# One block's four token sums on VectorE: two of them issued two readings later, two of them issued in the next product

## The chip, the cores and the metric

The kernel runs on one core of one Trainium2 chip. The metric is the time on the device of one execution, in microseconds; three executions of the kernel before took 588.06, 588.19 and 589.07 us, so its median is 588.19 us. Engine names below: PE is TensorE, DVE is VectorE, ACT is ScalarE, POOL is GpSimd, SP is the engine that issues most DMAs.

## The reference

`x` has 2 x 2048 tokens of 512 numbers; all is float32. One conditioned block is computed:

```python
emb = jnp.dot(jax.nn.silu(t), ada_w) + ada_b
shift_msa, scale_msa, gate_msa, shift_mlp, scale_mlp, gate_mlp = jnp.split(emb, 6, axis=-1)
norm = _ln(x) * (1.0 + scale_msa[:, None]) + shift_msa[:, None]
h = jax.nn.gelu(jnp.dot(norm, ssm_w1) + ssm_b1, approximate=False)
ssm_out = jnp.dot(h, ssm_w2) + ssm_b2
x = x + gate_msa[:, None] * ssm_out
norm2 = _ln(x) * (1.0 + scale_mlp[:, None]) + shift_mlp[:, None]
hf = jax.nn.gelu(jnp.dot(norm2, ff_w1) + ff_b1, approximate=True)
ff_out = jnp.dot(hf, ff_w2) + ff_b2
x = x + gate_mlp[:, None] * ff_out
```

The weights are 512 x 512 (`ssm_w1`, `ssm_w2`), 512 x 1024 (`ff_w1`) and 1024 x 512 (`ff_w2`).

## The kernel before

The 4096 tokens are cut into eight blocks of 512 (numbers 0 to 7). A block passes through four matrix products, named in the program by the tile that they write: hA (the first ssm product, class `First`), oA (the second, with the residual added to `x`, function `residual`), hC (the first feed-forward product) and oC (the second, with its residual). Each is done by a scheme of the Strassen kind: the operands are cut in quarters, seven products P1 to P7 of quarters or of sums of quarters are made in place of eight, and what they give is added up again. So each product needs sums of its operands beforehand. For the ssm input of a block these are the token sums: four additions or subtractions of quarters of the normalized, modulated tokens, each 128 partitions x 512 numbers. `Norm.summed` returns them as a list of four closures that call `cut_sum` (L348). In words, with q11 to q22 the quarters:

- sum 1: s0 = q12 - q11
- sum 2: s1 = q22 - s0
- sum 3: q12 = q22 - q12, in place
- sum 4: s2 = q21 - s1

`second_operands` says which product uses which: P1 takes q11, P5 takes s0, P6 takes s1, P2 takes q21, P7 takes q12 (as sum 3 left it), P3 takes q22, P4 takes s2.

The program has no scheduler of its own: the order of the instructions on each engine is the order in which the Python code issues them. `group` (L475) issues the seven products of one matrix product, four matmuls of 256 columns each; after each product it calls `after`, which issues the readings of that product's PSUM bank, and then runs the closures that were hung on this place with `hook`. The order of the products here is `CARRIED`: P1, P5, P6, P2, P7, P3, P4. The places, however, are named in the order of `ORDER`: P1, P2, P6, P5, P7, P3, P4. So place "P2" comes after product P5, place "P5" comes after product P2, and places "P1", "P6", "P7", "P3" and "P4" come after the products of the same names.

PSUM banks are shared: P1, P6, P7 and P4 accumulate in one tile (`py`), P5 and P3 in a second (`pv`), P2 in a third (`px`). In a residual, DVE reads a bank after each product but the first and adds it to `x` (L739); ACT copies P1's bank to P2's (L489). A product that adds to a bank must wait until the reading of the product before it in this bank is done: P7 waits for P6's reading, P3 for P5's, P4 for P7's.

The change lies in one place: round i = 5 of the loop over blocks (`ahead` is true there alone). The work around it, in order of issue:

- the hC products of block 5, in whose hooks block 7's tokens are normalized (L580), turned (L591) and moved by 16 DMAs on SP (L600);
- the oA residual of block 6. Behind its product P1, ACT modulates block 7's tokens (four instructions, L623), and POOL makes the sums that oC of block 5 needs (L348). On DVE are hung block 7's four token sums and, at "P3" and "P4", four bn_stats with bn_aggr of block 6 (L512, L513);
- the hA product of block 7 (`First`, L475), which takes the token sums. ACT copies P1 (L489) and reads P5 and P6 (L682), P2 (L692) and P4 (L708); DVE reads P7 (L701) and P3 (L704);
- the oC residual of block 5 (`residual_in_leaves`, L778 and L824), at whose start POOL works out block 6's scales (L548 to L566), makes four more sums (L348), and then four of hA.

The token sums of this block are the only ones from round 1 on that DVE makes; those of the other blocks are POOL's. Before, the four stand at the places "P6", "P6", "P5" and "P7" of the residual:

Of the kernel before, what the change touches and what calls it, by code (L numbers as in the profile page):

```python
# [140 lines left out]
def kernel(  # L141
# [16 lines left out]
    nc = tc.nc  # L158
# [279 lines left out]
    def seed(name, row, part, leaf=False):  # L438


        b, cols = (("y", row[:, : D // 2]), ("v", row[:, D // 2 :]))[part]
        t = ps_g.tile([P, 2, HT], F32, tag=b, name=f"p{b}_{name}_{len(seeds.get((name, b), ()))}")
        seeds.setdefault((name, b), []).append(t)
        if part == 1 and leaf:
            nc.scalar.copy(t[:, 0, :P], cols[:, :P])
        else:
            nc.scalar.copy(t, cols.unsqueeze(1).to_broadcast([P, 2, HT]))
# [45 lines left out]
    def hook(hooks, places, ops):  # L493

        for n, op in enumerate(ops):
            hooks.setdefault(places[min(n, len(places) - 1)], []).append(op)
# [226 lines left out]
    def residual(name, i, hops, wops, kdim, hooks, last=False, order=ORDER):  # L723

        xt = xs[i]
        F = D // 2
        q = {
            "11": xt[:, 0:2, :F],
            "12": xt[:, 0:2, F:],
            "21": xt[:, 2:4, :F],  # L730
            "22": xt[:, 2:4, F:],
        }
        dest = {"P1": "11", "P2": "11", "P6": "12", "P5": "22", "P7": "22", "P3": "12", "P4": "21"}

        def after(p, ps, js):
            if p == "P1" and order is CARRIED:
                return
            d = q[dest[p]][:, js]
            nc.vector.tensor_tensor(d, ps[BANK[p]][:, js], d, ALU.add)  # L739
            if last and p in ("P7", "P4"):  # L740
                s = slice(2 + js.start, 2 + js.stop)
                f = slice(F, D) if p == "P7" else slice(0, F)
                nc.sync.dma_start(out=out_blk[i][:, s, f], in_=xt[:, s, f])

        parted = ("P1", "P6", "P7", "P4") if last else ()
        places = ORDER if order is CARRIED else None
        group(name, kdim, hops, lambda p, j, k: wops[p][:, k, :], after, hooks, parted, order, places)
# [306 lines left out]
    def run(ops):  # L1054
        for op in ops:
            op()
# [4 lines left out]
    n1 = {0: Norm(0, 1), 1: Norm(1, 1)}  # L1061
# [65 lines left out]
    n1_sums = n1[0].summed(nc.vector)  # L1127
# [17 lines left out]
    hooks = {}  # L1145
# [12 lines left out]
    hooks = {}  # L1158
# [24 lines left out]
    n1_sums = n1[1].summed(nc.vector)  # L1183
    run(st[2:3] + n1_sums[:2] + st[3:])
    hooks = {}
# [19 lines left out]
    hooks = {}  # L1205
# [14 lines left out]
    hooks = {}  # L1220
# [25 lines left out]
    hooks = {}  # L1246
# [10 lines left out]
    hooks = {}  # L1257
# [7 lines left out]
    hooks = {}  # L1265
# [12 lines left out]
    for i in range(1, NBLK):  # L1278
# [4 lines left out]
        hooks = {}  # L1283
# [43 lines left out]
        hooks = {}  # L1327
# [12 lines left out]
        if nx2:  # L1340

            hook(hooks, ("P1",) if ahead else ("P7",), n1[i + 2].moved())
            if ahead:
                hook(hooks, ("P6", "P6", "P5", "P7"), n1[i + 2].summed(nc.vector, True))
            if i == 1:
                hook(hooks, ("P1", "P1", "P2", "P6"), later[:4])
            if fold:
                hook(hooks, ("P1", "P2", "P6", "P5"), fold[5:6] + fold[4:5] + later[:2])
            oC_seeds = [lambda p=p: seed(f"oC_{i}", gb[5], p, five) for p in range(2)]
            if not ahead:  # L1350
                hook(hooks, ("P2", "P6"), oC_seeds)
            n2[i + 1] = Norm(i + 1, 2)
            hook(hooks, ("P3", "P4"), n2[i + 1].stats())
            residual(f"oA_{i + 1}", i + 1, hA[i + 1], w2_ops, KD // 2, hooks, order=CARRIED)
            if ahead:
                hooks = {}
                hook(hooks, ("P2", "P6"), oC_seeds)
                hA[i + 2] = First(i + 2, n1[i + 2].ops, hooks, CARRIED, on_act=("P6", "P5"))
        else:
            for p in EARLY:  # L1360
                run(hooks.get(p, ()))
        leaf_fold, fold = (fold or i == 1) and later[2 if fold else 4 :], None

        hooks = {}
# [63 lines left out]
        hooks = {}  # L1428
# [63 lines left out]
```

## Time and profile before

| what | us |
|---|---|
| median of three executions | 588.19 (588.06 to 589.07) |
| the profiled execution, its whole time | 588.16 |
| the same execution, first to last instruction (span) | 586.4 |
| PE busy, 430 to 457 us of the span (27 us) | 25.61 |
| DVE busy in the same stretch | 14.92 |
| ACT busy in the same stretch | 12.24 |
| POOL busy in the same stretch | 22.29 |

The last four rows are from the view by stretches of time; the oA residual of block 6 and the hA product of block 7 lie in this stretch. Times in the profile's rows are microseconds from the first instruction. Durations on PE and DVE overlap a little with the next instruction, since the engines are pipelined: DVE's readings of 0.69 us start every 0.60 us when nothing holds them, and products of eight rows (four matmuls appear as eight) last 1.89 us but start every 1.73 us. The granted TensorE clock is 0.999 of full speed.

### The profile page before, as it was taken

The page shows a single profiled execution, that of the slowest core. Times are in us where ns is not written, and L with a number is a line of the kernel's source. Part 1 is how long each engine was busy: PE and PEld are TensorE (multiplying, and loading weights), DVE is VectorE, ACT ScalarE, POOL GpSimd, SP SyncE. Part 2 cuts the span into 40 slices and gives each one's busy share as a digit, 9 for nine tenths or more (in the row PEclk, how much of TensorE's full clock was granted, in tenths as well). Part 3 has the DMA queues.
Part 4 walks back from the last instruction along what each step waited for, and adds up shares of the span by engine and source line. Part 5 has one row for each costly group of instructions (what it writes and reads, how often), then busy time and mean ns, then how long its engine had stood idle before and what let it go on. Part 6 is the DMA issues. An engine that isn't in the chain of part 4 may idle for free.

```text
span 586.4 us, 9484 instructions
## 1 busy us (share of the span) xinstructions
PE 577.9 (99%) x3303; PEld 515.5 (88%) x3303; DVE 417.9 (71%) x752; ACT 263.1 (45%) x479; POOL 428.4 (73%) x518
## 2 busy tenths in 40 slices
PE   8999999999999999999999999999999999999997
PEld 5888888888899888998889988898887998899896
DVE  4978788987867375685756857883856366787676
ACT  2234357405642554435742588226663431731420
POOL 2875359999997938969688799998688445369351
PEclk9999999999999999999999999999999999999999
DMA  8990323302205403472033721153030330031002
GB/s 317 395 393 10 91 64 82 108 37 107 55 19 178 129 1 74 113 209 72 3 90 78 282 73 29 45 141 129 19 72 1 106 113 0 1 73 72 2 1 72
DMA packets 25243, 56.49 MB, mean 96 GB/s; under 512 B 4672, under 2 KB 5740, under 8 KB 23532
## 3 DMA queue, kind: packets, MB, share of 16 engines
q1 hardware_dynamic: 21856, 51.67, 27.7%
q10 hardware_dynamic: 3340, 4.22, 3.0%
q8 instruction: 26, 0.43, 0.3%
q14 instruction: 21, 0.17, 0.1%
HBM read 32.80 MB, written 8.40 MB: 70 GB/s over the span
## 4 chain that ended last, share of the span: by engine, by line
PE 91%; DVE 3%; DMA 3%; issue 1%; ACT 0%; SPq 0%; DVEq 0%
PE px_hC L985 10%; PE py_hA L475 9%; PE py_oA L475 9%; PE py_hC L985 8%; PE py_oC L778 8%; PE pv_hC L985 8%; PE pl_oC_P_y L824 8%; PE pl_oC_P_v L824 5%; PE pv_hA L475 4%; PE pv_oA L475 4%; PE pl_oC_P_x L824 3%; DMA ada<-in_L_cond_ada_w_dram 2%; PE py_hC L475 2%; PE py_oC L475 2%; PE px_oA L475 2%; PE px_hA L475 2%
## 5 line engine op out<-in xcount | busy, mean ns | idle before, releaser
L623 ACT ACTIVATE nT<-nT,mod,mod 128x512 f32<-128x512 f32 x32 | 23.4, 803 | 56.2 <-DMA nT<-blocks 40.1
L348 POOL TENSOR_TENSOR hSC<-hClo,hChi 128x512 f32<-128x512 f32 (+1 forms) x16 | 19.7, 1235 | 38.7 <-ACT hChi L980 33.3
L512 DVE BATCH_NORM_STATS2 st<-x 128x6 f32<-128x512 f32 x60 | 40.7, 678 | 5.4 <-DMA x<-in_x_dram 5.2
L923 POOL TENSOR_TENSOR forms<-forms 128x256 f32<-128x256 f32 x56 | 41.8, 746 | 3.3
L985 PE MATMUL py_hC<-forms,fw 128*128 128x256 f32 x168 | 41.0, 380 | 0.0
L1002 DVE TENSOR_TENSOR hClo<-hClo,py_hC 128x512 f32<-128x512 f32 x42 | 28.6, 684 | 15.3 <-ACT hClo L999 9.4
L985 PEld LDWEIGHTS py_hC<-forms,fw 128*128 128x128 f32 x168 | 31.7, 190 | 4.7 <-DVE hClo L1002 0.2
L623 ACT ACTIVATE x<-x,mod,mod 128x512 f32<-128x512 f32 x24 | 17.6, 802 | 32.1 <-DMA x<-blocks 32.1
L591 DVE STREAM_TRANSPOSE blocks<-nT 128x512 f32<-128x512 f32 x32 | 22.2, 705 | 13.5 <-ACT nT L580 13.5
L923 POOL TENSOR_TENSOR forms<-nT,forms 128x256 f32<-128x256 f32 x42 | 30.5, 748 | 1.8 <-PE pl_oC_P_v L824 1.3
L923 POOL TENSOR_TENSOR forms<-nT 128x256 f32<-128x256 f32 x14 | 10.4, 740 | 29.3 <-ACT nT L623 20.4
L1002 DVE TENSOR_TENSOR hChi<-hChi,pv_hC 128x512 f32<-128x512 f32 x35 | 23.2, 681 | 10.4 <-PE pv_hC L985 6.7
L580 ACT ACTIVATE nT<-x,nmr,rstd 128x512 f32<-128x512 f32 x32 | 24.1, 806 | 13.4 <-POOL nmr L566 13.4
L985 PE MATMUL px_hC<-forms,fw 128*128 128x256 f32 x112 | 27.6, 379 | 0.0
L980 ACT ACTIVATE hClo<-hClo,colsT 128x256 f32<-128x256 f32 x56 | 25.3, 498 | 5.0 <-DVE hClo L1002 4.8
L838 DVE TENSOR_TENSOR x<-pl_oC_P_y,x 128x256 f32<-128x256 f32 (+1 forms) x66 | 24.7, 374 | 3.0 <-PE pl_oC_P_y L824 1.3
L475 PE MATMUL py_oA<-w,hA 128*128 128x256 f32 x112 | 26.5, 379 | 0.0
L999 ACT ACTIVATE hChi<-py_hC 128x512 f32<-128x512 f32 x14 | 7.6, 593 | 41.1 <-PE py_hC L985 41.0
L980 ACT ACTIVATE hChi<-hChi,colsT 128x256 f32<-128x256 f32 x56 | 25.1, 496 | 1.9 <-DVE hChi L1002 1.9
L739 DVE TENSOR_TENSOR x<-py_oA,x 128x512 f32<-128x512 f32 x26 | 17.8, 686 | 11.2 <-PE py_oA L475 10.6
L778 PE MATMUL py_oC<-fw_s,hSC 128*128 128x256 f32 x112 | 25.3, 379 | 0.0
L739 DVE TENSOR_TENSOR x<-pv_oA,x 128x512 f32<-128x512 f32 x16 | 11.0, 687 | 20.1 <-PE pv_oA L475 9.0
(339 smaller groups left out, 1796.7 us busy)
## 6 DMA issues: line engine op xcount, KB each, us to landing
x<-in_x_dram SPq DMA_DIRECT2D x13, 1024.0 KB
out_dram<-x SPq DMA_DIRECT2D x14, 512.0 KB
ada<-in_L_cond_ada_w_dram SPq DMA_DIRECT2D x6, 1024.0 KB
x<-blocks SPq DMA_DIRECT2D x96, 64.0 KB
nT<-blocks SPq DMA_DIRECT2D x80, 64.0 KB
fw<-in_L_cond_ff_w_dram SPq DMA_DIRECT2D x2, 2048.0 KB
w<-in_L_cond_ssm_w_dram SPq DMA_DIRECT2D x3, 1024.0 KB
nT<-blocks ACTq DMA_DIRECT2D x48, 64.0 KB
```

The lines of the kernel that those rows point to most:

```text
L475: nc.tensor.matmul(ps[b][j * apart][:, j, :], lhs(p, j, k), rhs(p, j, k), start=(fresh and j * (not apart) == 0 and k == 0), stop=(p in (" ...
L512: nc.vector.bn_stats(st, xs[self.i][:, c, :])
L580: nc.scalar.activation(t, x_c, AF.Identity, bias=self.nmr[:, c : c + 1], scale=self.rstd[:, c : c + 1])
L623: nc.scalar.activation(dst, src, AF.Identity, bias=shift, scale=scale)
L739: nc.vector.tensor_tensor(d, ps[BANK[p]][:, js], d, ALU.add)
L778: yield lambda j=j, k=k: nc.tensor.matmul(ps[BANK[p]][:, j, :], hops(p, j, k), wops[p][:, k, :], start=False, stop=(k == kdim - 1), skip_g ...
L824: nc.tensor.matmul(t[:, n, :], hops.leaves[p][f][:, k, :], leaf_wops[p][f][:, k, :], start=room not in started, stop=(f in ("P2", "P3", "P ...
L838: nc.vector.tensor_tensor(d, src, d, ALU.add)
L923: eng.tensor_tensor(reg[d], reg[a], reg[b], ALU.add if f == "+" else ALU.subtract)
L980: nc.scalar.activation(h, h, AF.Gelu_apprx_tanh, bias=fb1T[:, m : m + 1])
L985: nc.tensor.matmul(ps[b][:, j, :], fa[ra][:, j * P : (j + 1) * P], fb[rb].rearrange("p a (c q) -> p c a q", q=Q), start=(fresh and j == 0) ...
L1002: nc.vector.tensor_tensor(dest(d), dest(d), ps[b], op)
```

## The change

Sums 1 and 2 move to the places "P5" and "P7" of the residual, which come after the readings of the products P2 and P7. Sums 3 and 4 leave the residual and move to the places "P1" and "P2" of the hA product, which come after its first and its second product. On DVE they then stand behind the last readings and all bn_stats of the residual. Nothing else changes: the number of instructions on each engine, their operands, the tiles and the DMAs stay.

```diff
             hook(hooks, ("P1",) if ahead else ("P7",), n1[i + 2].moved())
             if ahead:
-                hook(hooks, ("P6", "P6", "P5", "P7"), n1[i + 2].summed(nc.vector, True))
+                n1_sums = n1[i + 2].summed(nc.vector, True)
+                hook(hooks, ("P5", "P7"), n1_sums[:2])
             if i == 1:
                 hook(hooks, ("P1", "P1", "P2", "P6"), later[:4])
...
             if ahead:
                 hooks = {}
+                hook(hooks, ("P1", "P2"), n1_sums[2:])
                 hook(hooks, ("P2", "P6"), oC_seeds)
                 hA[i + 2] = First(i + 2, n1[i + 2].ops, hooks, CARRIED, on_act=("P6", "P5"))
```

DVE's order in this stretch, by the instruction streams of the two programs:

```
before: read P5, read P6, sum 1, sum 2, read P2, sum 3, read P7, sum 4, read P3, stats, read P4, stats x3, [hA] read P7, read P3
after:  read P5, read P6, read P2, sum 1, read P7, sum 2, read P3, stats, read P4, stats x3, sum 3, sum 4, [hA] read P7, read P3
```

## The prediction

> **What bounds the kernel now.** I began with the page's head, for the engine that fills the span:
>
> ```profile
> span 586.4 us, 9484 instructions
> PE 577.9 (99%) x3303; PEld 515.5 (88%) x3303; DVE 417.9 (71%) x752; ACT 263.1 (45%) x479; POOL 428.4 (73%) x518
> ```
>
> PE is busy in all but 8.5 us, and some of those lie at the two ends. Any gain must therefore be a hole in PE's work, and any loss a new one. Next came PE's own waits over the whole run:
>
> ```profile
> PE py_oA L475 <- DVE x L739: 1.4, 1, 1.4
> PE idle L1078 <- POOL ident masks.py:199: 1.3, 1, 1.3
> PE rowsT L1087 <- DMA fw_t<-in_L_cond_ff_b_dram: 0.7, 1, 0.7
> ```
>
> The others, two of them shown, belong to the start of the run. The first is the largest and occurs once: a product of an oA residual waits for a reading by DVE. The timeline of PE puts it into the residual that the diff touches:
>
> ```profile
> 437.83 1.89 PE L475 MATMUL py_oA<-w,hA 128*128 128x256 f32 x8
> 439.55 1.89 PE L475 MATMUL pv_oA<-w,hSA 128*128 128x256 f32 x8
> 442.83 1.99 PE L475 MATMUL py_oA<-w_s,hA 128*128 128x256 f32 x8 [1.39 <-DVE x L739]
> 444.66 1.89 PE L475 MATMUL py_hA<-x,w 128*128 128x256 f32 x8
> ```
>
> These are P7, P3 and P4 of the residual and P1 of hA. P4 accumulates where P7 did, so it waits for P7's reading. Why that reading is late stands in DVE's timeline:
>
> ```profile
> 436.37 0.69 DVE L739 TENSOR_TENSOR x<-py_oA,x 128x512 f32<-128x512 f32 x1 [0.94 <-PE py_oA L475]
> 437.32 1.50 DVE L348 TENSOR_TENSOR nS<-x 128x512 f32<-128x512 f32 x1 [0.26 <-ACT x L623]
> 438.93 1.57 DVE L348 TENSOR_TENSOR nS<-x,nS 128x512 f32<-128x512 f32 x1
> 440.42 0.68 DVE L739 TENSOR_TENSOR x<-px_oA,x 128x512 f32<-128x512 f32 x1
> 441.02 1.16 DVE L348 TENSOR_TENSOR x<-x 128x512 f32<-128x512 f32 x1
> 442.10 0.68 DVE L739 TENSOR_TENSOR x<-py_oA,x 128x512 f32<-128x512 f32 x1
> ...
> 443.78 0.68 DVE L739 TENSOR_TENSOR x<-pv_oA,x 128x512 f32<-128x512 f32 x1
> ...
> 445.32 0.66 DVE L739 TENSOR_TENSOR x<-py_oA,x 128x512 f32<-128x512 f32 x1
> ...
> 448.20 0.18 DVE L513 BATCH_NORM_AGGREGATE mv<-st 128x2 f32<-128x6 f32 x1
> 453.59 0.69 DVE L701 TENSOR_TENSOR hA<-py_hA,hA 128x512 f32<-128x512 f32 x1 [5.22 <-PE py_hA L475]
> ```
>
> P7's last matmul ends at 437.83 + 1.89 = 439.72, but DVE reads it only at 442.10, because sums 1, 2 and 3 stand ahead of it; from 437.32 on DVE has no idle time. P4 starts 0.73 after the reading does. The last row shows that DVE then idles 5.22 us: there is room later.
>
> **The hole, sized.** Undisturbed, P4 would start 1.73 after P3, at 439.55 + 1.73 = 441.28, and hA's P1 at 443.01. It starts at 444.66. So 1.65 us can be won: 1.55 of late start (442.83 - 441.28), and 0.10 because the first matmul after the hole is longer (1.99 against 1.89).
>
> **The change, step by step.** DVE executes the same instructions, so nothing is added or removed in work; only the queue order moves.
>
> Reading of P2: its matmuls end at 436.10 + 1.89 = 437.99 (timeline). Readings start 0.11 after that (P6: 434.37 + 1.89 = 436.26, read at 436.37), so at 438.10 instead of 440.42, and DVE is free for the next at 438.70.
>
> Sum 1 starts then. Its tokens are ready: ACT's modulation of the first two of four parts is what released it at 437.24 before. Its length is not certain, since the same shape on DVE took 0.69 (L348 at 559.81, with POOL idle) to 1.75 (L348 at 566.54); I take its own 1.50, for POOL is again in the same run of sums:
>
> ```profile
> 437.00 1.26 POOL L348 TENSOR_TENSOR forms<-hChi 128x512 f32<-128x512 f32 x1
> 438.35 1.60 POOL L348 TENSOR_TENSOR forms<-forms,hChi 128x512 f32<-128x512 f32 x1
> 439.91 1.72 POOL L348 TENSOR_TENSOR hChi<-hChi 128x512 f32<-128x512 f32 x1
> ```
>
> The next instruction starts 1.49 later (438.93 to 440.42 behind sum 2), so P7's reading starts at 440.19, later than its data (439.83), and P4 may start at 440.19 + 0.73 = 440.92. PE is free at 441.28: 0.36 to spare, and the hole closes. Bounds: with 0.69 the reading starts at 439.83 and P4 may go at 440.56; with 1.75 P4 may go at 441.17. One more cost is unseen: sum 1 carries waits on eight DMA queues, ACT and POOL, which were spent while it waited anyway. Semaphore instructions on DVE take 0.021 here, so at most 0.21 more, if none hides beside the reading. Both worst cases together give 441.38: 0.10 of the hole stays. A gain beyond 1.65 is excluded at this point, since PE cannot start earlier than behind P3.
>
> [...]
>
> Sum 2 follows P7's reading at about 440.8 and ends by 442.4 (1.57). It is needed by hA's P6; hA's products now start at 443.01, 444.74 (P5, needs sum 1), 446.47 (P6), 448.19 (P2), 449.92 (P7), 451.65 (P3) and 453.38 (P4). Four us to spare. P3's reading stands behind sum 2, at 442.3 instead of 443.78; P4's follows 1.54 later as before (443.78 to 445.32), at 443.8; the last aggregate ends 3.06 behind that (445.32 to 448.38), at 446.9. So the scales on POOL, which wait for it, start earlier by 1.5 too.
>
> Sum 3 starts at 446.9 and ends between 447.6 and 448.7 (0.69 to 1.75); hA's P7 needs it at 449.92, so 1.2 are left at worst. I cost it at nothing: DVE's 5.22 us of idle time hide it, and without that cover each us past 449.92 would be a us on PE. Sum 4 ends by 450.4, needed at 453.38. Behind both on DVE waits hA's P7 reading, whose data come at 449.92 + 1.89 + 0.11 = 451.92, and whose bank P4 needs; 1.5 to spare.
>
> POOL: two of the four DVE sums no longer fall among its sums from 437 to 447; they meet its scales (448.47 to 451.45 before). If each stretches POOL by up to 0.5 (1.72 against 1.27 undisturbed), its run ends no later against PE than before within 1 us. Its next customers are far: the sums of hA that follow end at 461.8 and are used by oA of block 7 at 481.
>
> **Does the gain reach the end?** In the chain of waits PE follows PE without a gap from 444.8 to 570.4; then DVE's readings of the last residual end the run, released by PE. What lies beside it starts from PE's progress: the load of block 7's tokens is issued at 456.98, when hA's P4 has ended (456.91), and block 6's turning, DMAs, modulation (472.31) and POOL forms (475.32 to 491.14) start from copies and readings in oC. All should come 1.65 earlier with it. SP's queue is not touched.
>
> **Sum.** Span 586.4 - 1.65 = 584.75; the execution lies 588.16 - 586.4 = 1.76 above its span, so 586.51. The profiled execution is 0.03 below the median of the three runs: 586.5.
>
> **The rivals.** A change of this kernel under 0.2% (1.18 us, so from 587.01 to 589.37) cannot be told from none.
>
> *A. Part of the hole stays, chance 0.08.* Sum 1 still stands ahead of P7's reading. If ACT's modulated tokens come late or POOL holds sum 1 through two of its sums (2 x 1.27 + 0.69 = 3.2), the reading starts at 441.8 and P4 at 442.5: hole 1.2 and the longer first matmul 0.1, time 587.8; with half of that 587.2. Against it: no sum of this shape in the trace took over 1.75, and the tokens were there 1.46 earlier.
>
> *B. The wait moves instead of going, chance 0.07.* PE comes 1.65 earlier to something not tied to it, and waits there: time 588.2. For it: POOL's forms end only at 491.14, 0.23 before the first hC product of block 6 starts. Against it: those products use the forms one by one, so the last is needed much later, and PE's waits name nothing near.
>
> *C. Slower: sum 3 comes too late for hA's P7, chance 0.06.* It now stands behind four readings and all bn_stats. From 449.92 on it makes a hole, from 451.57 the change is a loss. If POOL's scales (2.98 from 448.47 to 451.45) and two of its sums (2.54) went first, it would end at 446.9 + 2.98 + 2.54 + 0.69 = 453.1: a hole of 3.2, and 586.5 + 3.2 = 589.7. Against it: sums 1 to 3 were held at most 0.9 each, and this takes 5.5.
>
> **Chances and range.** The forecast has the remaining 0.79: 586.1 to 587.0, from the 0.10 of its bounds and the spread of the two lower runs. A and B give no measurable change (0.15), C slower (0.06). The range takes in the quicker half of A: 586.1 to 587.4.
>
> **What would show it.** In the profile after, PE's waits should lose the 1.4 line, P4 should start 1.73 after P3, P7's reading should start near 440.2, sum 3 should end before 448.7 with hA's P7 1.73 behind P2, and the end should come 1.65 earlier. A wait of PE at P4 speaks for A, one at hA's P7 for C, one behind 444 elsewhere for B. The forecast is wrong if the span's end does not move with hA's start.

## The result, and the profile after

The changed kernel takes 586.55 us, the median of seven executions (586.46 to 586.68), against 588.22 us for the kernel before (588.06 to 589.07, seven executions): a ratio of 0.997, 95% interval 0.9958 to 0.9981. That is 1.67 us less. The forecast was 586.5.

The head of the page after:

```profile
span 584.7 us, 9487 instructions
PE 577.8 (99%) x3303; PEld 515.5 (88%) x3303; DVE 416.3 (71%) x752; ACT 263.2 (45%) x479; POOL 428.2 (73%) x518
```

PE's busy time is unchanged (577.8 against 577.9), while the span is 1.7 shorter: what went is idle time of PE. Each engine has as many busy instructions as before; the three more in the total are semaphore instructions, two on PE and one on DVE. The waits of PE over the whole run, after:

```profile
PE idle L1078 <- POOL ident masks.py:199: 1.3, 1, 1.3
PE rowsT L1087 <- DMA fw_t<-in_L_cond_ff_b_dram: 1.1, 1, 1.1
```

The 1.4 us of `py_oA` for DVE is gone, and no wait has come in its place; both lines left belong to the start. PE's timeline shows the same products as in the prediction (P7, P3 and P4 of the residual, P1 of hA; columns: start, length, engine, line, operation):

```profile
437.81 1.89 PE L475 MATMUL py_oA<-w,hA 128*128 128x256 f32 x8
439.54 1.89 PE L475 MATMUL pv_oA<-w,hSA 128*128 128x256 f32 x8
441.27 1.89 PE L475 MATMUL py_oA<-w_s,hA 128*128 128x256 f32 x8
443.00 1.89 PE L475 MATMUL py_hA<-x,w 128*128 128x256 f32 x8
```

They follow each other every 1.73 us, and P1 of hA starts at 443.00, not 444.66. On DVE:

```profile
438.02 0.69 DVE L739 TENSOR_TENSOR x<-px_oA,x 128x512 f32<-128x512 f32 x1 [0.97 <-PE px_oA L475]
438.62 1.54 DVE L348 TENSOR_TENSOR nS<-x 128x512 f32<-128x512 f32 x1
440.09 0.68 DVE L739 TENSOR_TENSOR x<-py_oA,x 128x512 f32<-128x512 f32 x1
440.69 1.15 DVE L348 TENSOR_TENSOR nS<-x,nS 128x512 f32<-128x512 f32 x1
...
446.29 0.66 DVE L348 TENSOR_TENSOR x<-x 128x512 f32<-128x512 f32 x1
446.86 0.68 DVE L348 TENSOR_TENSOR nS<-x,nS 128x512 f32<-128x512 f32 x1
451.93 0.69 DVE L701 TENSOR_TENSOR hA<-py_hA,hA 128x512 f32<-128x512 f32 x1 [4.38 <-PE py_hA L475]
```

P7's reading starts at 440.09 (442.10 before) with one sum ahead of it. Sums 3 and 4 end by 447.54, and DVE still idles 4.38 us before hA's P7 is there to be read.

### The profile page after: what moved, and what is told of

It reads as the page before. It is cut to its first block, busy times and chain, and to the rows that moved or that the text cites. A ratio compares the mean times of both kernels' runs of the same rounds, so it can differ in the third digit from the quotient of the medians.

```text
span 584.7 us, 9487 instructions
## 1 busy us (share of the span) xinstructions
PE 577.8 (99%) x3303; PEld 515.5 (88%) x3303; DVE 416.3 (71%) x752; ACT 263.2 (45%) x479; POOL 428.2 (73%) x518
## 4 chain that ended last, share of the span: by engine, by line
PE 93%; DMA 3%; DVE 2%; issue 0%; DVEq 0%
PE px_hC L985 10%; PE py_oA L475 9%; PE py_hA L475 9%; PE py_hC L985 8%; PE py_oC L778 8%; PE pv_hC L985 8%; PE pl_oC_P_y L824 8%; PE pv_oA L475 5%; PE pl_oC_P_v L824 5%; PE pv_hA L475 4%; PE pl_oC_P_x L824 3%; PE py_oC L475 2%; PE py_hC L475 2%; PE px_oA L475 2%; DMA ada<-in_L_cond_ada_w_dram 2%; PE px_hA L475 2%
## 5 line engine op out<-in xcount | busy, mean ns | idle before, releaser
L778 PE MATMUL py_oC<-fw,hClo 128*128 128x256 f32 x112 | 25.3, 379 | 0.0
```

What stands on the lines that cost most here:

```text
L778: yield lambda j=j, k=k: nc.tensor.matmul(ps[BANK[p]][:, j, :], hops(p, j, k), wops[p][:, k, :], start=False, stop=(k == kdim - 1), skip_g ...
```

## The experiments

Three questions: is the number of sums ahead of P7's reading what makes the hole, and do both halves of the change (sums 1 and 2; sums 3 and 4) matter; why are the sums so long; and how late may sum 3 be.

**How many sums stand ahead of P7's reading.** Four kernels differ from the changed one only in the places of the sums.

Two ahead, both behind P2's reading:

```diff
-                hook(hooks, ("P5", "P7"), n1_sums[:2])
+                hook(hooks, ("P5",), n1_sums[:2])
```

> Sums 1 and 2 both stand between the readings of P2 and P7; sums 3 and 4 as in the changed kernel. Theory (the hole in PE is P7's reading pushed past 440.55 by the sums ahead of it): sum 1 ends its turn at 440.09 as in the changed kernel's profile, sum 2 then meets a POOL sum (440.1 to 441.3) and P7's reading starts at 441.6 to 441.8, so P4 starts at 442.3 to 442.5: a hole of 1.1 to 1.2 and 587.6 to 587.9. Rival (what counts is that sums 3 and 4 left the residual): 586.5.

The second half of the change alone:

```diff
-                hook(hooks, ("P5", "P7"), n1_sums[:2])
+                hook(hooks, ("P6",), n1_sums[:2])
```

> Only the second half of the change: sums 1 and 2 stay behind P6's reading as before, sums 3 and 4 go into hA. Theory: up to P2's reading all is as before (440.42), then P7's reading follows at 441.0 instead of 442.10, since sum 3 no longer stands between; P4 starts at 441.75, a hole of 0.5 and 0.1 for its longer first matmul: 587.1. Rival (moving sums 3 and 4 brings the whole gain): 586.5. Rival (it brings nothing): 588.2.

The first half alone:

```diff
-                hook(hooks, ("P5", "P7"), n1_sums[:2])
+                hook(hooks, ("P5", "P7"), n1_sums)
...
-                hook(hooks, ("P1", "P2"), n1_sums[2:])
```

> Only the first half of the change: sums 1 and 2 as in the changed kernel, sums 3 and 4 right behind sum 2 in the residual, ahead of P3's reading. Theory: nothing that PE waits for stands behind P7's reading, so PE has no hole and the time is 586.5; bn_stats end some 2 us later than in the changed kernel, and POOL's scales with them. Rival (sums 3 and 4 must leave the residual, since they delay the readings of P3 and P4 and the scales): 587.0 or more.

No sum ahead:

```diff
-                hook(hooks, ("P5", "P7"), n1_sums[:2])
+                hook(hooks, ("P7", "P3"), n1_sums[:2])
```

> Sum 1 moves behind P7's reading too, sum 2 behind P3's; sums 3 and 4 as in the changed kernel. Theory: with one sum ahead P7's reading already ends before PE is free, so taking it away as well brings nothing: 586.5, P7's reading at 439.8. Rival (the sum that is left ahead still costs something): 586.4 or less.

Times are medians of 7 to 10 executions; the starts are those of each one's profiled execution.

| kernel | sums ahead of P7's reading | this reading starts | P4 starts | PE waits | time (ratio to before, 95%) |
|---|---|---|---|---|---|
| before | 3 | 442.10 | 442.83 | 1.39 | 588.22 |
| two ahead | 2 | 441.59 | 442.32 | 1.05 | 587.96 (0.9987 to 1.0005) |
| second half alone | 2, both ahead of P2's reading too | 441.07 | 441.80 | 0.32 | 587.15 (0.9974 to 0.9993) |
| changed | 1 | 440.09 | 441.27 | 0 | 586.55 (0.9958 to 0.9981) |
| first half alone | 1 | 440.19 | 441.38 | 0 | 586.63 (0.9962 to 0.9984) |
| none ahead | 0 | 439.80 | 441.33 | 0 | 586.56 (0.9963 to 0.9983) |

The product P6 of the residual starts between 434.20 and 434.48 in these profiles, ahead of anything that differs, so starts of different kernels compare to within 0.3 us. The time follows the start of P7's reading until P4 no longer waits for it, and then stays. The first half of the change brings the whole gain, although the sums in the residual then delay bn_stats and POOL's scales (these start at 449.37, against 446.46 in the changed kernel): nothing near waits for those. The second half alone brings about two thirds (588.22 - 587.15 = 1.07 of 1.67), by taking sum 3 from ahead of P7's reading. It doesn't add to the first half.

In the kernel with the second half alone the hole is small, and one reads its price from two rows of PE (P3 and P4); the same two rows with two ahead stand below them:

```profile
439.59 1.89 PE L475 MATMUL pv_oA<-w,hSA 128*128 128x256 f32 x8
441.80 1.99 PE L475 MATMUL py_oA<-w_s,hA 128*128 128x256 f32 x8 [0.32 <-DVE x L739]
```

```profile
439.38 1.89 PE L475 MATMUL pv_oA<-w,hSA 128*128 128x256 f32 x8
442.32 1.99 PE L475 MATMUL py_oA<-w_s,hA 128*128 128x256 f32 x8 [1.05 <-DVE x L739]
```

With the second half alone P4 is due at 439.59 + 1.73 = 441.32; 0.48 of lateness and the 0.10 of the longer matmul make 0.58, and 586.55 + 0.58 = 587.13. The idle time that the row names (0.32) is less than the lateness (0.48), since products overlap: they last 1.89 us and start every 1.73.

Two ahead was expected at 587.6 to 587.9 and gave a median of 587.96, with executions from 587.65 (the profiled one) to 588.56; its interval can't tell it from before. So this kernel's time doesn't confirm the theory, only its rows do: P4 is 442.32 - 441.11 = 1.21 late (441.11 is 439.38 + 1.73), which with 0.10 makes 587.86. In the profiled execution P6 starts 0.16 earlier than in the changed kernel (434.20 against 434.36), which is most of the way from 587.86 to 587.65. Why the executions spread over 0.9 us, where those of the changed kernel spread over 0.2, is not settled.

**Why the sums take 1.2 to 1.6 us.** The rows of before (1.16 to 1.57 us, each beside a sum of POOL) let one think that POOL's sums hold them up. Two kernels leave POOL's eight leaf sums of block 5 out, with the old and with the new order:

```diff
-        else:
+        elif not ahead:
             hook(hooks, ("P5",), sums24)
...
-        elif nx2:
+        elif nx2 and not ahead:
             hook(hooks, ("P7",), sums7)
```

Old order:

> The order of the kernel before, but POOL's eight leaf sums of block 5 (sums of hChi's and hClo's quarters into forms) are left out, so POOL idles from 437.0 to the scales; the output of block 5 is not the reference's. If the token sums are long because POOL's sums hold them up, each now takes 0.69: sum 1 at 437.3, sum 2 at 438.7 when ACT's fourth modulation is done, P2's reading at 439.3, sum 3 at 439.9, P7's reading at 440.5, early enough for P4 at 441.28. No hole, 586.5, with the old order. Rival (they are long by their own access patterns, or the order alone makes the hole): sums of 1.2 to 1.6 again, a hole of 1.4 again, 588.2.

Measured: 586.55 us, a ratio to before of 0.996 to 0.9982. DVE, old order, POOL free:

```profile
437.39 0.69 DVE L348 TENSOR_TENSOR nS<-x 128x512 f32<-128x512 f32 x1 [0.25 <-ACT x L623]
438.75 0.69 DVE L348 TENSOR_TENSOR nS<-x,nS 128x512 f32<-128x512 f32 x1 [0.66 <-ACT x L623]
439.36 0.68 DVE L739 TENSOR_TENSOR x<-px_oA,x 128x512 f32<-128x512 f32 x1
439.96 0.68 DVE L348 TENSOR_TENSOR x<-x 128x512 f32<-128x512 f32 x1
440.56 0.68 DVE L739 TENSOR_TENSOR x<-py_oA,x 128x512 f32<-128x512 f32 x1
```

Every sum takes 0.68 or 0.69, sum 2 now waits for ACT, P7's reading starts at 440.56, and P4 at 441.36. With three sums ahead of the reading there is no hole. So the old order cost 1.67 us only together with POOL's sums in the same stretch: the hole needs both.

New order:

> The changed kernel with the same eight POOL sums of block 5 left out, so its output of block 5 is not the reference's. If POOL holds the token sums, sums 1 and 2 take 0.69 in place of 1.54 and 1.15 and the time stays at 586.5, as PE has no hole to lose. Rival (POOL's sums cost time elsewhere in this stretch too): below 586.3.

Measured: 586.55 us (0.9959 to 0.9983), with sums 1 and 2 at 0.68 each: the shorter sums bring nothing more, as PE has no hole left here.

**How late sum 3 may be.** Four kernels put more bn_stats, whose results nothing uses, on DVE ahead of sum 3:

```diff
+                def fill():
+                    st = small.tile([P, nc.vector.BN_STATS_DIM], F32, tag="st", name="st_fill")
+                    nc.vector.bn_stats(st, xs[i + 1][:, 0, :])
+
-                hook(hooks, ("P1", "P2"), n1_sums[2:])
+                hook(hooks, ("P1",) * 5 + ("P2",), [fill] * 4 + n1_sums[2:])
```

The edit shown adds four. The second kernel adds twelve (`("P1",) * 13` and `[fill] * 12`), and eight and ten, further down, follow the same form:

> The changed kernel with four more bn_stats on DVE ahead of sum 3 (their results are used by nothing). They take 0.6 to 0.7 each, so sum 3 ends 2.4 to 2.8 later, at 449.4 to 449.8. hA's P7 is due at 449.90, so by the theory that sum 3 has some 2.9 us of cover nothing is lost: 586.5 to 586.7. Rival (the cover is the 1.2 us that the prediction kept as its worst bound): a hole of 1.2 to 1.6, about 588.

> The changed kernel with twelve more bn_stats on DVE ahead of sum 3 (used by nothing), 7.2 to 8.4 us. Sum 3 ends at 454.1 to 455.4, hA's P7 waits for it 4.3 to 5.5 us and the time is 590.8 to 592.1: past the cover each us on DVE is a us of PE. Rival (later work has slack that takes a part of the hole back): 589 or less.

Four gave 586.51: sum 3 ended at 449.44 and hA's P7 started on time at 450.03, 1.73 after P2. The rows are DVE's of sum 3 and PE's of P2 and P7 of hA:

```profile
448.76 0.68 DVE L348 TENSOR_TENSOR x<-x 128x512 f32<-128x512 f32 x1
448.30 1.89 PE L475 MATMUL px_hA<-x,w 128*128 128x256 f32 x8
450.03 1.89 PE L475 MATMUL py_hA<-x,w 128*128 128x256 f32 x8
```

Twelve gave 593.81, 7.26 more than the changed kernel, above what either theory expected. PE's rows of P2, P7, P3 and P4 of hA with twelve:

```profile
448.24 1.89 PE L475 MATMUL px_hA<-x,w 128*128 128x256 f32 x8
455.25 3.75 PE L475 MATMUL py_hA<-x,w 128*128 128x256 f32 x8 [5.12 <-DVE x L348]
458.79 2.76 PE L475 MATMUL pv_hA<-x,w_s 128*128 128x256 f32 x8
461.38 1.89 PE L475 MATMUL py_hA<-nS,w 128*128 128x256 f32 x8
```

P7 is 455.25 - 449.97 = 5.28 late, as expected, but it and P3 also run slower, and P4 is 461.38 - 453.42 = 7.96 late. The expectation "each us on DVE is a us of PE" was too low. What was missing is the granted clock, the share of its full speed at which TensorE is clocked: it was 0.50 in every stretch of 1 us from 454 to 460. Two more kernels asked from which length of hole it falls. Eight and ten bn_stats:

> Eight more bn_stats ahead of sum 3. From the run with twelve (0.59 each), sum 3 starts at 451.1, ends at 451.8 to 452.8 by what POOL holds, and hA's P7 starts at 451.9 to 452.9 instead of 449.96: a hole of 1.9 to 2.9. If a hole costs its own length and no more: 588.5 to 589.5. If the granted clock falls to 0.50 behind a hole of this length as it did behind the one of 5.1: some 2 us more, 590.5 to 591.5.

> Ten more bn_stats ahead of sum 3, which then starts at 452.3 and ends at 453.0 to 454.0; hA's P7 starts at 453.1 to 454.1, a hole of 3.1 to 4.1. If the clock holds: 589.7 to 590.7. If it falls to 0.50 as with twelve: some 2 us more, 591.7 to 592.7.

Eight gave 591.12 (589.52 to 591.36), as expected for a falling clock. Ten gave 593.05 (592.38 to 593.75), above what either case expected. PE's rows of P2, P7 and P4 of hA with eight:

```profile
448.28 1.89 PE L475 MATMUL px_hA<-x,w 128*128 128x256 f32 x8
452.88 2.99 PE L475 MATMUL py_hA<-x,w 128*128 128x256 f32 x8 [2.70 <-DVE x L348]
458.09 1.89 PE L475 MATMUL py_hA<-nS,w 128*128 128x256 f32 x8
```

In the view by stretches of 1 us (columns: stretch, length, busy time and instructions of PE, PEld, DVE, ACT and POOL, granted clock, DMA share, GB/s), with eight, then with ten and with twelve:

```profile
452.00:453.00 1.00, 0.12 (x1) 0.15 (x2) 1.00 (x2) 0.39 (x2) 1.00 (x2) 1.00 0.00 0
453.00:454.00 1.00, 1.00 (x5) 0.83 (x6) 1.00 (x1) 0.00 (x0) 1.00 (x2) 0.83 0.00 0
454.00:455.00 1.00, 1.00 (x4) 0.81 (x3) 0.40 (x1) 0.00 (x0) 1.00 (x1) 0.50 0.00 0
457.00:458.00 1.00, 1.00 (x6) 0.90 (x5) 0.00 (x0) 0.35 (x1) 0.00 (x0) 0.96 0.00 0
```

```profile
454.00:455.00 1.00, 0.94 (x3) 0.78 (x4) 1.00 (x1) 0.00 (x0) 1.00 (x1) 0.57 0.00 0
457.00:458.00 1.00, 1.00 (x5) 0.76 (x5) 0.15 (x1) 0.00 (x0) 0.00 (x0) 0.72 0.00 0
```

```profile
453.00:454.00 1.00, 0.00 (x0) 0.00 (x0) 1.00 (x2) 0.00 (x0) 1.00 (x2) 0.85 0.00 0
460.00:461.00 1.00, 1.00 (x5) 0.79 (x4) 0.00 (x0) 0.49 (x1) 0.00 (x0) 0.73 0.00 0
```

A mean clock of 0.83 in a stretch of 1 us is 0.34 us at 0.50, so with eight the clock falls at 453.66, 0.8 us behind the hole's end, with PE already at work again, and comes back 3.4 us later. Worked out in the same way, it falls at 454.14 with ten (0.1 behind the hole's end) and at 453.70 with twelve, still inside the hole; the words "behind the one of 5.1" in the expectation for eight are wrong there. A hole of 2.70 us (eight) thus cost 4.6 in the profiled execution: P7 starts 2.87 late (452.88 - 450.01), and P4 another 1.76.

In the table, all columns but the last are of the profiled execution.

| bn_stats added | sum 3 ends | hA's P7 starts | PE waits | clock at 0.50 for | time of this execution | median |
|---|---|---|---|---|---|---|
| 0 (changed) | 446.95 | 449.90 | 0 | 0 | 586.51 | 586.55 |
| 4 | 449.44 | 450.03 | 0 | 0 | 586.64 | 586.51 |
| 8 | 452.73 | 452.88 | 2.70 | 3.4 | 591.28 | 591.12 |
| 10 | 453.91 | 454.06 | 3.92 | 3.4 | 592.44 | 593.05 |
| 12 | 455.10 | 455.25 | 5.12 | 6.8 | 594.55 | 593.81 |

From eight on, sum 3 itself takes 1.61 to 1.65 instead of 0.66 (none added) and 0.68 (four): it now runs beside POOL's sums, which last from 449.57 to 455.53 with eight.

## Why the prediction was right

**The hole and its size.** The prediction took 1.65 us from the starts of P1 of hA (444.66 against 443.01). P1 now starts at 443.00, the span is 1.7 shorter and the median 1.67 lower. The rows of the two kernels between, with 1.05 and 0.32 us of waiting, show that this size comes from the start of P7's reading, and the four kernels with other places show that the sums ahead of it set this start. The prediction didn't say which part of the change brings the gain: the first half alone does.

**Sum 1 ahead of P7's reading.** Expected 1.50 long, the reading at 440.19; measured 1.54 and 440.09, as P2's reading had started 0.08 earlier than expected (438.02, not 438.10). The bound of 0.21 for semaphore waits was too small and had no effect: four of the semaphore instructions ahead of sum 1 took 0.050 each, not 0.021, and the run of them lasted from 438.03 to 438.55, but all of it lay beside P2's reading. Sum 1 starts 0.60 behind the start of that reading, as sum 2 does behind P7's (440.09 and 440.69). The kernel with no sum ahead shows that the 0.36 us to spare were real: it is no faster.

**The length of the sums beside POOL.** The token sums took 0.66 to 0.69 where no sum of POOL ran, 0.99 to 1.75 beside POOL's sums. Some of POOL's own sums of this shape were longer as well: before, 1.27 at 435.77, with no token sum beside it, and 1.72 at 439.91 and 441.58, beside sums 2 to 4. By what mechanism they lengthen each other no run shows. The prediction treated this length as a bound on a term; in truth it is one of the two things that make the hole, beside the order, as the old order without POOL's sums shows.

**Sums 2 to 4.** They were costed at nothing, rightly. Sum 2 took 1.15, not 1.57. Sum 3 was to end between 447.6 and 448.7 and ended at 446.95: it started at 446.29, not 446.9, mostly since sum 2 ahead of it was shorter, and it took 0.66, as POOL made no sum then, only the tiny scales, the first of them 0.17 behind its start:

```profile
446.46 0.54 POOL L548 TENSOR_SCALAR ve<-mv 128x4 f32<-128x4 f32 x1 [0.62 <-DVE mv L513]
447.08 1.36 POOL L550 TENSOR_TENSOR r<-ve,minus_half 128x4 f32<-128x4 f32 x1
```

These two took 0.19 and 1.04 before: beside the token sums POOL took 0.7 us longer, for which nothing waited. The cover was 2.95 us instead of the 1.2 that stood as the worst case; four bn_stats (2.4 us) went into it at no cost.

**The way to the end.** All that the prediction tied to PE's progress moved with it: the load of block 7's tokens is issued at 455.31 (456.98 before), block 6's modulation starts at 470.69 (472.31).

**The rivals.** A (part of the hole stays) is what the second half alone and two ahead show; the change goes past it. That POOL holds a sum through two of its own (3.2 us), as A supposed, no run shows: of block 7's token sums none took over 1.75, and the longest sum of this shape on DVE before took 1.77 (at 572.03), not 1.75. B (the wait moves) falls with PE's waits. C (sum 3 too late) did not happen; its mechanism exists. Sum 3 ending at 449.44 cost nothing and ending at 452.73 made hA's P7 late, so the runs bracket the limit that the prediction put at 449.92. But its price was too low: it counted a us for a us, and in the profiled execution with eight bn_stats 2.87 us of lateness cost 4.6, since the clock fell to 0.50 too.

No kernel that was run is measurably faster than the changed one.

## What to carry to other kernels

When a product waits for a reading in a bank that it shares, look at what stands ahead of that reading in the reading engine's queue; work that is needed only later belongs behind it, as far as the engine's next idle time. Before moving anything, ask why the instructions ahead are long: the token sums on DVE took up to two and a half times as long beside sums on POOL (1.75 against 0.69), and with POOL idle the same order cost nothing (586.55 us). And one sum ahead of the reading was harmless, so count to the point where the wait ends, not to zero.

## What the runs showed of the hardware

A hole in PE's work can cost more than its length: one of 2.70 us cost 4.6. Waits of PE of 0.32 to 1.39 us left the granted clock at 1.00 in the profiled executions. With waits of 2.70, 3.92 and 5.12 us it fell to 0.50, 3.5 to 4.0 us after PE had gone idle: behind the end of the two shorter holes, inside the longest. It stayed there for 3.4, 3.4 and 6.8 us; four matmuls (eight rows) that lay wholly in this time took 3.75 us instead of 1.89.

The same hole doesn't always cost the same. The record has the mean granted clock of every execution: 0.998 to 1.000 in all kernels without a hole beyond 1.39 us, and 3.4 us at 0.50 in some 590 us lower it by 0.003 (an estimate). With eight bn_stats the executions of 589.52 and 590.05 us have 1.000, the four from 590.96 to 591.36 have 0.995 to 0.997. So in two of six the clock seems not to have fallen, and these are 2.97 and 3.50 us slower than the changed kernel, where the four others are 4.41 to 4.81 slower. With ten, two executions (592.38 and 592.44) have 0.997, and two (593.67 and 593.75) have 0.994 and 0.992, as with 6.8 us at 0.50; these two lift the median above the expectation. No trace shows one of the executions that differ from the profiled ones.

Which length of hole it takes, no run here shows: one of 1.39 us left the clock at 1.00, one of 2.70 us was enough in the profiled execution, and none was run between them. Why the kernel with eight seems to lose the clock in four executions and not in two is not shown either.
